# Value projections from seven half-size products, with their sums stored, in a transformer block on one core

## The chip, the cores and the metric

The kernel runs on one core of a Trainium2 chip. The core has a matrix engine (TensorE, PE in the profile; its weight loads are PEld), VectorE (DVE), ScalarE (ACT), GpSimd (POOL) and SyncE (SP), which here only issues transfers, and 16 DMA engines that they share. Each engine works through its own instructions in order. The metric is the time of one execution on the device in microseconds; several runs are taken and their median is compared.

## What is computed

One transformer block in fp32 over 2048 tokens of 512 features. Six rows of 512 numbers (sa, ca, ga, sb, cb, gb) come from a small product and modulate the block.

```python
h = layernorm(x) * (1 + ca) + sa
q, k, v = h @ Q_w + Q_b, h @ K_w + K_b, h @ V_w + V_b     # 16 heads of 128
attn = softmax(causal(q @ k.T / sqrt(128))) @ v
x = x + ga * (sum over heads of attn @ O_w + O_b)
h = layernorm(x) * (1 + cb) + sb
x = x + gb * (64 routed experts, 4 per token + 2 shared experts)(h)
```

The change concerns the values `h @ V_w`, part of the softmax, and where sb, cb and gb are kept until the second half needs them.

## The kernel before

**Layout.** The normalised input lies transposed in four tiles `hTs[j]` of 512 tokens each: 128 partitions, 4 chunks of features, 512 tokens. `Ts[b]` holds four sums and differences of quarters of a pair of such tiles, made once by VectorE (`sum_h`). They serve the query and key projections: `project` computes queries and keys of one head for 1024 tokens from seven half-size products where the plain way has eight (Strassen's scheme, with sums of the weights made by `sum_w`). Its first product is copied by ScalarE, and the other six are added up by VectorE.

**Values.** Two heads make a group; there are eight groups. `make_v` (lines 419 to 434) computes 128 tokens of both heads of a group: four products with a block of `hTs` as the stationary operand and 256 columns of the weights `wv` streaming, summed in one PSUM buffer, and a copy by ScalarE. A group takes 16 such units. The results lie in tiles `v` of 512 tokens by 256 columns.

**Steps.** Attention runs head by head, and each head in five steps, numbered 0 to 4, over pairs of query tiles (`BATCHES`: pair 7; 6; 5 and 0; 4 and 1; 3 and 2). While a step's weighted values are computed, the softmax of the step two further on is made (`softmax_work(n + 2)`), so the softmax work seen in steps 3 and 4 of a head is that of steps 0 and 1 of the next head, the widest ones. For a chunk of up to 1024 scores TensorE writes the products into one of two score buffers in PSUM, VectorE adds the mask where it is needed and takes the maximum, ScalarE takes the exponential, which frees the buffer. A row of more than 1024 scores has two chunks, and a correction factor `fix` joins them. Then the probabilities are divided by their sum: in steps 0 and 1 by VectorE (line 489), in the others by ScalarE (`flush_shares`, line 716). At a step's end `swap` issues the transfers that exchange 32-row blocks of the probabilities (SP's queue, 8 transfers), and VectorE transposes within the blocks (`turn`, line 556) in two halves, at 0.55 and 0.8 of the next step. Only then can TensorE use them as the moving operand of the weighted values (line 574).

**Filling.** Beside these, each step has units that are not tied to it (`fillers`, line 596). In steps 0, 1 and 2 they are five, five and four of the 14 products of the next head's `project`. In steps 3 and 4 they are four and four units of `make_v` for the next group: an even head makes tokens 0 to 1023, an odd head the rest. In the last two heads there is no further group.

**Order.** The schedule is written by hand. `merge` takes the streams of a step (softmax, weighted values, filling), and always emits the next unit of that stream which has emitted the smallest share of its cost; at a tie the stream named first goes first. Marks run an extra piece when a share of the whole has been emitted: the transposes at 0.55 and 0.8, and `sum_w` at 0.3 of step 4, which has ScalarE scale the query weights in place (line 199) and VectorE add and subtract weights (lines 201 to 204). The products of `project`, of `make_v` and of `late_mod` share two PSUM buffers (tag `mm`).

**Modulation rows.** `late_mod` (line 625) computes the row i of the modulation and leaves it on all partitions in one of the tiles ga, sb, gb, cb: ga in head 2, sb in head 4, gb in head 6, cb in head 14. `gate` limits ga and gb with six VectorE operations, in head 2 and head 6.

The attention is followed by the output projection (from about 1690 us), the routing, and the experts (to the end).

Of the kernel before, what the change touches and what calls it, by code (L numbers as in the profile page):

```python
# [9 lines left out]
F32 = mybir.dt.float32  # L10
# [13 lines left out]
def adaln_block_kernel(  # L24
# [49 lines left out]
    silc = const.tile([P, DC, P], F32)  # L74
    ga = const.tile([P, D], F32)
    cb = const.tile([P, D], F32)
    sb = const.tile([P, D], F32)
    gb = const.tile([P, D], F32)
    atd = dram.tile([H, DH, N], F32)
    h2d = dram.tile([N, D], F32)  # L80
    ybd = dram.tile([E * CAP, D], F32)
# [39 lines left out]
    with ExitStack() as att:  # L121
# [41 lines left out]
        def plain(b, j, dst):  # L163

            w = heads[0][b]
            ps = psA.tile([P, 512], F32, name="pqk", tag="mm")
            for k in range(DC):
                nc.tensor.matmul(
                    out=ps,
                    lhsT=w[:, k, :],  # L170
                    rhs=hTs[j][:, k, :],
                    start=(k == 0),
                    stop=(k == DC - 1),
                )
# [19 lines left out]

        sums_w = {}

        def sum_w(hd):
            wq, wk = heads[hd]
            nc.scalar.activation(wq, wq, AF.Identity, scale=scale)
            sw = qkw.tile([P, 4, 2, DH], F32, name="sw")  # L200
            nc.vector.tensor_add(sw[:, 0], wk[:, 0:2, :], wk[:, 2:4, :])
            nc.vector.tensor_sub(sw[:, 1], sw[:, 0], wq[:, 0:2, :])
# [59 lines left out]
        with tc.tile_pool(name="pre", bufs=1) as pre, tc.manual_schedule():  # L262
# [130 lines left out]
                nc.vector.tensor_scalar(silc[:, k, :], ones, sg[:, k : k + 1], None, ALU.mult)  # L393
            plain(1, NB - 1, kts[0, NB - 1])
            plain(0, 3, qts[0, 3])
            sum_w(1)
            sum_h(1)

# [15 lines left out]
        def spare(g):  # L414

            both = [vp.tile([P, 4, HG * DH], F32, name=f"v{at}") for at in free[g]]
            return [b.rearrange("p i d -> p (i d)") for b in both]

        def make_v(g, t):

# [38 lines left out]
        def softmax_tile(hd, s, pr, i, pb):  # L459

            qi = 2 * pr + i
            width = (qi + 1) * P
            nch = (width + SC - 1) // SC
            RB = blocks_of(s)
            r0 = first_block(s, pr) + i * (2 * pr + 1)
            rows = pb[:, : 4 * RB * 32].rearrange("q (b r k) -> q r b k", b=4, k=32)
            cols = pb[:, : 4 * RB * 32].rearrange("q (b r) -> q b r", b=4)  # L470
            box = {}

            def normalise():
                nm, sums = box["nm"], box["sums"]
                rs = smp.tile([P, 2], F32, name="rs")
                if nch == 1:
                    nc.vector.reciprocal(rs[:, 0:1], sums[:, 0:1])
                else:
                    fix = box["fix"]
                    nc.vector.scalar_tensor_tensor(  # L480
                        rs[:, 1:2], sums[:, 0:1], fix, sums[:, 1:2], ALU.mult, ALU.add
                    )
                    nc.vector.reciprocal(rs[:, 1:2], rs[:, 1:2])
                    nc.vector.tensor_mul(rs[:, 0:1], rs[:, 1:2], fix)  # L484
                for n in range(nch):
                    a = (r0 + n * SC // P) * 32
                    b = (r0 + min(width, (n + 1) * SC) // P) * 32
                    if s < 2:
                        nc.vector.tensor_scalar(
                            cols[:, :, a:b], cols[:, :, a:b], rs[:, n : n + 1], None, ALU.mult  # L490
                        )
                    else:
                        shares.append((cols[:, :, a:b], rs[:, n : n + 1]))

            def chunk(n):
                c0 = n * SC
                w = min(SC, width - c0)
                q = qts[hd, qi // 4][:, (qi % 4) * P : (qi % 4 + 1) * P]
                ps = psA.tile([P, SC], F32, name="ps", tag="sc")
                for o in range(0, w, 512):  # L500
                    wo = min(512, w - o)
                    nc.tensor.matmul(  # L502
                        out=ps[:, o : o + wo],
                        lhsT=q,
                        rhs=kts[hd, (c0 + o) // 512][:, :wo],
                        start=True,
                        stop=True,
                    )
# [12 lines left out]
                nc.scalar.activation(  # L521
                    rows[:, r0 + c0 // P : r0 + (c0 + w) // P],
                    ps[:, :w].rearrange("q (r b k) -> q r b k", b=4, k=32),
                    AF.Exp,
                    bias=nm[:, n : n + 1],
                    accum_out=sums[:, n : n + 1],
                )
# [68 lines left out]
        def fillers(hd, s):  # L596

            g = hd // HG
            if s < 3:
                if s == 0 and hd + 1 < H:  # L600
                    ahead.extend(project(hd + 1, 1) + project(hd + 1, 0))
                n = 4 if s == 2 else 5
                out = ahead[:n]
                del ahead[:n]
                return out
            if g + 1 == NG:
                return []
            t0 = (hd % HG) * NP + 4 * (s - 3)
            return [(1024, lambda t=t: make_v(g + 1, t)) for t in range(t0, t0 + 4)]

        ahead = []

# [12 lines left out]
        def late_mod(i, dst):  # L625

            pm = psA.tile([P, D], F32, name="pm", tag="mm")
            for k in range(DC):
                nc.tensor.matmul(
                    out=pm, lhsT=silc[:, k, :], rhs=mods[i][k], start=(k == 0), stop=(k == DC - 1)  # L630
                )
            if i == 4:
                nc.vector.tensor_scalar_add(dst, pm, 1.0)
            else:
                nc.vector.tensor_copy(dst, pm)

        MOD_LOADS = {(2, 0): 2, (4, 0): 3, (6, 0): 5, (14, 0): 4}
        MOD_ROWS = {(2, 2): (2, ga), (4, 2): (3, sb), (6, 2): (5, gb), (14, 3): (4, cb)}


        PLACES = (2, 3, 0, 1)
# [95 lines left out]
        with tc.manual_schedule():  # L737
# [10 lines left out]
            for n, (hd, s) in enumerate(steps):  # L748
# [7 lines left out]
                    load_mod(MOD_LOADS[hd, s], hd // HG)  # L756
                if (hd, s) in MOD_ROWS:
                    fill.append((2048, lambda m=MOD_ROWS[hd, s]: late_mod(*m)))
                if (hd, s) in ((2, 3), (6, 3)):
                    mag = qkw.tile([P, 512], F32, name="p_")  # L760
                    gate(mag, ga if hd == 2 else gb)
                if (hd, s) == (14, 1):
                    fill.insert(2, (0, lambda: load_wo(0)))
                if (hd, s) == (14, 2):
# [30 lines left out]
                if outs:  # L795
                    upto = 8 if hd < H - 1 else (14, 14, 14, 10)[s]
                    fill += outs[:upto]
                    del outs[:upto]
                streams = [weighted_values(hd, s, turned.pop(n)), fill]
                if n + 2 < len(steps):  # L800
                    streams.insert(0, softmax_work(n + 2))
                marks = [(f, lambda i=i: scale_wo(i)) for f, i in WO_SCALES.get((hd, s), ())]
                if s == 4 and hd + 2 < H:
                    marks.append((0.3, lambda: sum_w(hd + 2)))
                if n + 1 < len(steps):
                    marks.append((0.55, lambda: turn(n + 1, 0)))
# [277 lines left out]
    with ExitStack() as ex:  # L1084
# [403 lines left out]
```

## Time and profile before

| | |
|---|---|
| median of three runs | 2420.02 us (2419.19 to 2422.03) |
| the profiled execution | 2419.9 us |
| its span, first to last instruction | 2418.1 us |
| TensorE busy | 2363.9 us |
| VectorE busy | 1511.8 us |
| ScalarE busy | 828.8 us |
| value products (line 427), 1024 records | 240.8 us busy |
| copies of values (line 434), 128 | 46.1 us busy |
| between 98 and 1560 us: TensorE, VectorE, ScalarE busy | 1445.6, 992.7, 625.4 us |

The profile is that of one execution. Each group of instructions has its line, engine, operation, the names of what it writes and reads, its shape, its count, the busy time and the mean length of one, then the idle time of its engine just before, and what ended it. Matrix products are pipelined: the length of one includes the time in which the next has already begun, so what a product costs is read from the distance of starts. An fp32 product shows as two records.

### The profile page before, as it was taken

How to read it: one execution, taken by the hardware profiler on the slowest of the kernel's cores; microseconds unless marked ns; L12 is line 12 of the kernel's file. 1: busy time of each engine (PE TensorE's matmuls, PEld its weight loads, DVE VectorE, ACT ScalarE, POOL GpSimd, SP SyncE). 2: the span in 40 equal slices, each digit the busy share in tenths (PEclk: the TensorE clock that was granted, in tenths of full speed). 3: DMA queues.
4: the chain of work that ended last, by engine and by line, in shares of the span. 5: the costliest groups of instructions: out<-in, count | busy, mean ns of one | idle time of the engine just before them, and what ended most of it. 6: DMA issues, size and time to landing. Idle time of an engine off the chain costs nothing. (4 is left out here: it accounts for less than half of the span.)

```text
span 2418.1 us, 26181 instructions
## 1 busy us (share of the span) xinstructions
PE 2363.9 (98%) x8406; PEld 1500.2 (62%) x8406; DVE 1511.8 (63%) x2878; ACT 828.8 (34%) x1737; POOL 217.8 (9%) x286
## 2 busy tenths in 40 slices
PE   7899999999999999999999999999999999999999
PEld 3566666666666665666666656555444476876743
DVE  5366676676776766767667676764655563654564
ACT  3243443443444444444443444432211221222200
POOL 0000000000000000000000000000000111111073
PEclk9999999999999999999999999999999999999999
DMA  4224544454454443444445444665432368778664
GB/s 140 62 71 116 122 120 108 97 144 102 103 128 108 115 119 95 114 111 103 121 97 124 114 101 120 164 191 140 137 122 87 101 203 250 232 215 244 187 199 153
DMA packets 223681, 325.22 MB, mean 134 GB/s; under 512 B 31876, under 2 KB 138424, under 8 KB 223544
## 3 DMA queue, kind: packets, MB, share of 16 engines
q1 hardware_dynamic: 196664, 252.21, 40.6%
q0 software_dynamic: 17664, 54.54, 7.5%
q10 hardware_dynamic: 9216, 16.78, 1.8%
q8 instruction: 68, 1.11, 0.2%
q14 instruction: 69, 0.57, 0.1%
HBM read 138.86 MB, written 41.94 MB: 75 GB/s over the span
## 5 line engine op out<-in xcount | busy, mean ns | idle before, releaser
L521 ACT ACTIVATE p<-ps,nm 128x1024 f32<-128x1024 f32 (+7 forms) x384 | 332.0, 864 | 879.8 <-DVE nm L519 407.7
L574 PE MATMUL po<-pt,v 128*128 128x256 f32 (+1 forms) x2304 | 571.1, 368 | 16.7 <-DVE pt L556 15.0
L574 PEld LDWEIGHTS po<-pt,v 128*128 128x128 f32 x2304 | 426.6, 190 | 254.5 <-issue 184.1
L502 PE MATMUL ps<-kt,qt 128*128 128x512 f32 (+3 forms) x1280 | 530.9, 531 | 5.8 <-ACT p L521 4.0
L515 DVE TENSOR_REDUCE nm<-ps 128x1 f32<-128x1024 f32 (+7 forms) x384 | 347.5, 908 | 36.1 <-PE ps L502 27.3
L556 DVE STREAM_TRANSPOSE pt<-pt 128x1664 f32<-128x1664 f32 (+2 forms) x160 | 317.8, 1987 | 54.5 <-DMA pt<-p 53.7
L502 PEld LDWEIGHTS ps<-kt,qt 128*128 128x128 f32 x1280 | 233.7, 190 | 172.6 <-issue 137.8
L427 PE MATMUL pv<-wv,hT 128*128 128x256 f32 x1024 | 240.8, 379 | 2.2 <-ACT v L434 2.2
L588 POOL DMA_DIRECT2D atd<-at x128 | 74.3, 584 | 1612.5 <-ACT at L583 1589.4
L427 PEld LDWEIGHTS pv<-wv,hT 128*128 128x128 f32 x1024 | 194.4, 190 | 31.2 <-ACT v L434 3.0
L716 ACT ACTIVATE p<-p,rs 128x1024 f32<-128x1024 f32 (+7 forms) x256 | 200.0, 805 | 6.2 <-DVE rs L484 6.0
L514 DVE TENSOR_TENSOR ps<-ps,causal 128x128 f32<-128x128 f32 x256 | 74.2, 290 | 166.4 <-PE ps L502 163.3
L1058 PE MATMUL pso<-hT,T 128*128 128x512 f32 x384 | 175.4, 602 | 0.0
L217 PE MATMUL pqk<-T,sw 128*128 128x512 f32 x360 | 169.2, 592 | 0.0
L1350 PE MATMUL pse<-wgu,xbT 128*128 128x256 f32 x512 | 121.1, 379 | 0.0
L1058 PEld LDWEIGHTS pso<-hT,T 128*128 128x128 f32 x384 | 70.1, 192 | 72.1 <-issue 71.3
L217 PE MATMUL pqk<-hT,wq 128*128 128x512 f32 x240 | 114.2, 599 | 0.0
L1267 PE MATMUL psd<-wsd,hs 128*128 128x512 f32 x256 | 111.5, 592 | 0.0
L1350 PEld LDWEIGHTS pse<-wgu,xbT 128*128 128x128 f32 x512 | 93.8, 190 | 11.7 <-issue 1.0
L217 PEld LDWEIGHTS pqk<-T,sw 128*128 128x128 f32 x360 | 68.4, 190 | 47.7 <-issue 43.0
L1333 POOL DMA_INDIRECT xb<-h2d,tok x64 | 65.1, 1018 | 302.1 <-PE tpx L1343 273.0
L1345 ACT COPY xbT<-tpx 128x512 f32<-128x512 f32 x64 | 37.4, 586 | 146.0 <-DVE y L1373 54.4
(365 smaller groups left out, 2342.0 us busy)
## 6 DMA issues: line engine op xcount, KB each, us to landing
pt<-p SPq DMA_DIRECT2D x768, 104.0 KB, 2.2
pt<-p SPq DMA_DIRECT2D x256, 124.0 KB, 2.3
pt<-p SPq DMA_DIRECT2D x256, 108.0 KB, 2.2
atd<-at POOLq DMA_DIRECT2D x128, 128.0 KB, 2.2
wgu<-in_L_ffn_Wg_dram SPq DMA_DIRECT2D x64, 256.0 KB, 4.1
wgu<-in_L_ffn_Wu_dram SPq DMA_DIRECT2D x64, 256.0 KB, 4.6
wd<-in_L_ffn_Wd_dram SPq DMA_DIRECT2D x64, 256.0 KB, 3.7
ybd<-y ACTq DMA_DIRECT2D x64, 256.0 KB, 3.8
```

The costliest lines, as they stand in the source:

```text
L217: nc.tensor.matmul(out=ps, lhsT=l[:, k], rhs=r[:, k], start=(k == 0), stop=(k == 1))
L427: nc.tensor.matmul(out=ps, lhsT=hTs[t // 4][:, k, (t % 4) * P : (t % 4 + 1) * P], rhs=wv[:, k].rearrange("p i d -> p (i d)"), start=(k == ...
L502: nc.tensor.matmul(out=ps[:, o : o + wo], lhsT=q, rhs=kts[hd, (c0 + o) // 512][:, :wo], start=True, stop=True,)
L515: nc.vector.tensor_reduce(nm[:, n : n + 1], ps[:, :w], AX.X, ALU.max, negate=True)
L521: nc.scalar.activation(rows[:, r0 + c0 // P : r0 + (c0 + w) // P], ps[:, :w].rearrange("q (r b k) -> q r b k", b=4, k=32), AF.Exp, bias=nm ...
L556: nc.vector.transpose(part, part)
L574: nc.tensor.matmul(out=po if wide else po[:, P:], lhsT=vts[g, kt // 4][:, kt % 4, hh * DH : (hh + 1) * DH], rhs=rows[:, r : r + last + 1 : ...
L588: nc.gpsimd.dma_start(out=atd[hd, :, o * 256 : (o + 1) * 256], in_=at[:, m])
L716: nc.scalar.activation(part, part, AF.Identity, scale=r)
L1058: nc.tensor.matmul(out=ps, lhsT=abs_[pr][:, hd, i * P : (i + 1) * P], rhs=wos[hd // 4][:, hd % 4, :], start=(hd == 0), stop=(hd == H - 1),)
L1267: nc.tensor.matmul(out=ps, lhsT=hsh[b, f][:, i * P : (i + 1) * P], rhs=wsd[:, f, :], start=(f == 0), stop=(f == NHC - 1),)
L1350: nc.tensor.matmul(out=ps, lhsT=xts[e][:, k, :], rhs=weights[e][:, k].rearrange("p i h -> p (i h)"), start=(k == 0), stop=(k == DC - 1),)
```

## The change

Values of groups 1 to 7 are computed by the seven products as queries and keys are. For each head of the pair, `values` makes 1024 tokens of both heads of the group: the two halves of the tokens, of the features and the two heads give the quarters. Each product has four blocks of 128 tokens as the stationary operand, two halves of the feature quarter and 128 columns of one head's weights (or of a stored sum) streaming. ScalarE copies the first product, and VectorE adds up the other six with seven additions. `value_sums` makes four sums of the group's weights, once a group, in step 3 of the even head. Three products run in step 3 and four in step 4. Group 0 stays with `make_v`.

The sums lie in `sgb`, which is the room of the rows sb and gb, and an intermediate result in `cb`. Therefore the rows 3 and 5 are computed in `cb` at the same places as before, written to DRAM (`modd`), and read back into `sgb` at the start of head 14; gb is limited in step 2 of head 15.

Of the two wide tiles of steps 0 and 1, the one made first (i = 1) is normalised by ScalarE; the second stays with VectorE. The scaling of the query weights moves from 0.3 to 0.05 of step 4. In `merge` the filling now stands ahead of the weighted values in every step.

```diff
-    sb = const.tile([P, D], F32)
-    gb = const.tile([P, D], F32)
+    sgb = const.tile([P, 2, D], F32)
+    sb, gb = sgb[:, 0], sgb[:, 1]
+    modd = dram.tile([2, D], F32)
...
+        def scale_w(hd):
+            wq = heads[hd][0]
+            nc.scalar.activation(wq, wq, AF.Identity, scale=scale)
+
         def sum_w(hd):
             wq, wk = heads[hd]
-            nc.scalar.activation(wq, wq, AF.Identity, scale=scale)
...
+        def value_sums(g):
+            wv = groups[g]
+            s = sgb.rearrange("p a (j k d) -> p (a j) k d", j=2, k=2)
+            nc.vector.tensor_add(s[:, 0], wv[:, 0:2, 1], wv[:, 2:4, 1])
+            nc.vector.tensor_sub(s[:, 1], s[:, 0], wv[:, 0:2, 0])
+            nc.vector.tensor_sub(s[:, 2], wv[:, 0:2, 0], wv[:, 0:2, 1])
+            nc.vector.tensor_sub(s[:, 3], wv[:, 2:4, 0], s[:, 1])
+            return s
+
+        def values(g, b, s):
...
+            def product(l, r):
+                ps = psA.tile([P, 4, DH], F32, name="pv", tag="mm")
+                for n in range(4):
+                    for k in range(2):
+                        nc.tensor.matmul(
+                            out=ps[:, n], lhsT=l[:, k, n * P : (n + 1) * P], rhs=r[:, k],
+                            start=(k == 0), stop=(k == 1),
+                        )
+                return ps
...
+            def first():
+                box["p"] = qkw.tile([P, 512], F32, name="p_").rearrange("p (t d) -> p t d", t=4)
+                nc.scalar.copy(box["p"], product(hTs[i][:, 0:2], wv[:, 0:2, 0]))
+
+            def second():
+                nc.vector.tensor_add(u, box["p"], product(T[:, 1], s[:, 1]))
+
+            def third():
+                place(i)
+                nc.vector.tensor_add(of(i, 1), u, product(T[:, 2], s[:, 2]))
+
+            def fourth():
+                place(j)
+                ps = product(T[:, 0], s[:, 0])
+                nc.vector.tensor_add(of(j, 1), of(i, 1), ps)
+                nc.vector.tensor_add(of(j, 0), u, ps)
+
+            def fifth():
+                nc.vector.tensor_sub(of(i, 1), of(i, 1), product(T[:, 3], wv[:, 2:4, 1]))
+
+            def sixth():
+                nc.vector.tensor_add(of(j, 0), of(j, 0), product(hTs[j][:, 2:4], s[:, 3]))
+
+            def seventh():
+                nc.vector.tensor_add(
+                    of(i, 0), box["p"], product(hTs[i][:, 2:4], wv[:, 2:4, 0])
+                )
...
-                    if s < 2:
+                    if s < 2 and i == 0:
                         nc.vector.tensor_scalar(
...
-            t0 = (hd % HG) * NP + 4 * (s - 3)
-            return [(1024, lambda t=t: make_v(g + 1, t)) for t in range(t0, t0 + 4)]
+            if s == 3:
+                if hd % HG == 0:
+                    sums_v[0] = value_sums(g + 1)
+                behind.extend(values(g + 1, hd % HG, sums_v[0]))
+            out = behind[: s]
+            del behind[: s]
+            return out
...
+            if i in (3, 5):
+                nc.sync.dma_start(out=modd[i // 5 : i // 5 + 1, :], in_=dst[0:1, :])
...
-        MOD_ROWS = {(2, 2): (2, ga), (4, 2): (3, sb), (6, 2): (5, gb), (14, 3): (4, cb)}
+        MOD_ROWS = {(2, 2): (2, ga), (4, 2): (3, cb), (6, 2): (5, cb), (14, 3): (4, cb)}
...
-                if (hd, s) in ((2, 3), (6, 3)):
+                if (hd, s) in ((2, 3), (15, 2)):
...
+                if (hd, s) == (14, 0):
+                    nc.sync.dma_start(out=sgb, in_=modd.partition_broadcast(P))
...
-                streams = [weighted_values(hd, s, turned.pop(n)), fill]
+                streams = [fill, weighted_values(hd, s, turned.pop(n))]
...
                 if s == 4 and hd + 2 < H:
+                    marks.append((0.05, lambda: scale_w(hd + 2)))
                     marks.append((0.3, lambda: sum_w(hd + 2)))
```

More of the change, by code (lines that the diff above doesn't have):

```diff
@@ L395, in adaln_block_kernel @@
             plain(0, 3, qts[0, 3])
+            scale_w(1)
             sum_w(1)
@@ L417, in spare, with place, of @@
             return [b.rearrange("p i d -> p (i d)") for b in both]
+        def value_sums(g):
[7 more added lines that the diff above has]
+        def values(g, b, s):
+            i, j = 2 * b, 2 * b + 1
+            T = Ts[b]
+            wv = groups[g]
+            u = cb.rearrange("p (t d) -> p t d", t=4)
+            box = {}
+            def product(l, r):
[7 more added lines that the diff above has]
+                return ps
+            def place(j):
+                vts[g, j] = vp.tile([P, 4, HG * DH], F32, name=f"v{vplace[g][j]}")
+            def of(j, hh):
+                return vts[g, j][:, :, hh * DH : (hh + 1) * DH]
+            def first():
[19 more added lines that the diff above has]
+                )
+            return [(1024, f) for f in (first, second, third, fourth, fifth, sixth, seventh)]
@@ L607, in fillers @@
                 return []
-            t0 = (hd % HG) * NP + 4 * (s - 3)
-            return [(1024, lambda t=t: make_v(g + 1, t)) for t in range(t0, t0 + 4)]
+            if s == 3:
[5 more added lines that the diff above has]
+            return out
         ahead = []
+        behind = []
+        sums_v = {}
         mods = {}
```

## The prediction

> **What bounds the kernel now.** I began with the page: busy time of each engine, then the waits of TensorE, then the stretches of the attention.
>
> The page's first lines:
>
> ```profile
> span 2418.1 us, 26181 instructions
> ...
> PE 2363.9 (98%) x8406; PEld 1500.2 (62%) x8406; DVE 1511.8 (63%) x2878; ACT 828.8 (34%) x1737; POOL 217.8 (9%) x286
> ```
>
> TensorE is busy 98% of the span, VectorE 63%. A busy share alone can hide stalls, so I took the waits of TensorE between 150 and 1560 us, where the value products of groups 1 to 7 lie (who waited for whom: total us, times, longest):
>
> ```profile
> PE po L574 <- DVE pt L556: 7.0, 9, 1.6
> PE ps L502 <- ACT p L521: 3.0, 6, 0.9
> ```
>
> Ten microseconds in 1410: TensorE sets the pace there, and a change in time has to come from its instructions or from new waits of these two kinds. The stretches of one odd head (head 7, steps 3 and 4, then head 8, step 0) show what the others have left; columns are the stretch, its length, busy PE, PEld, DVE, ACT, POOL, the granted clock, DMA share, GB/s:
>
> ```profile
> 872.10:890.30 18.20, 18.20 (x74) 13.24 (x73) 10.45 (x15) 7.56 (x18) 1.07 (x2) 1.00 0.65 166
> 890.30:910.40 20.10, 18.84 (x80) 14.13 (x78) 14.19 (x24) 6.95 (x18) 1.28 (x2) 1.00 0.49 115
> 910.40:930.40 20.00, 20.00 (x65) 12.02 (x65) 15.04 (x29) 8.85 (x22) 1.22 (x2) 1.00 0.43 102
> ```
>
> The clock is full. VectorE has 8 us free in step 3 and 6 in step 4; ScalarE has 11 or more.
>
> **Part 1: seven products for eight.** Removed, for groups 1 to 7 (group 0 keeps the old way): 7 x 64 products of 256 columns. Each fp32 product is two records of the profile (the line has x1024 for 8 x 64). How far apart records start, I read from the timeline of TensorE (start, length, instruction, count):
>
> ```profile
> 902.56 1.89 PE L427 MATMUL pv<-wv,hT 128*128 128x256 f32 x8
> 904.29 0.59 PE L574 MATMUL po<-pt,v 128*128 128x256 f32 x2
> ```
>
> Eight records of 256 columns take 904.29 - 902.56 = 1.73 us, 0.216 each (the mean of 379 ns includes overlap). Removed: 896 x 0.216 = 193.5 us.
>
> Added: 7 x 14 = 98 products, each of 4 token blocks x 2 halves of 128 columns, so 16 records, each with a stationary block of its own. The columns fall to 7/8, the records rise from 896 to 1568, and so do the weight loads. Nothing before runs 16 such records on end; the nearest rows:
>
> ```profile
> 1759.02 0.60 PE L890 MATMUL tp<-ident,h 128*128 128x128 f32 x4
> 1759.46 3.60 PE L1058 MATMUL pso<-hT,T 128*128 128x512 f32 x8
> 1762.89 1.00 PE L899 MATMUL pl<-wr,h2T 128*128 128x64 f32 x8
> ```
>
> Four 128-column transposes, each with another block, start every 0.109 us (0.44 for four). Eight fp32 records of only 64 columns, each with another block, start 0.111 to 0.112 apart after the first, though their columns would need half of that: this is the pace of loading a 128x128 fp32 block. Here a rule speaks against the change: the Trainium skill ("TensorE: Matmul & The Clock Gate", LDWEIGHTS) puts a load at the number of stationary columns / 1.2 ns, however few columns then stream, 107 ns for 128. With 256 columns a load has 216 ns to hide in, with 128 none to spare. By the rule the stream still decides, 0.109: 1568 x 0.109 = 170.9, a gain of 22.6 us. By the row of 64 columns loading decides, 0.112: 1568 x 0.112 = 175.6, a gain of **17.9 us**. I take the row, as its records are fp32 products with distinct blocks; 22.6 stays as the good end. The bad end, loads not hidden at all (190 ns each, the PEld row): 298 us, 104 lost; the 64-column run excludes it nearly.
>
> The gain lies in step 3, which goes from four units of 1.73 to three of 1.79 (-1.5 us); step 4 keeps four (+0.25).
>
> **Part 2: the results move from ScalarE to VectorE.** ScalarE loses 16 copies of 368 ns a group and gets two of 128x512. VectorE gets for each of 14 heads seven additions of 128x512 from PSUM; the same form in the query products takes 668 to 688 ns:
>
> ```profile
> L244 DVE TENSOR_TENSOR qt<-qt,pqk 128x512 f32<-128x512 f32 x30 | 20.3, 678 | 0.0
> L489 DVE TENSOR_SCALAR p<-p,rs 128x1024 f32<-128x1024 f32 x80 | 58.8, 752 | 2.3
> L716 ACT ACTIVATE p<-p,rs 128x1024 f32<-128x1024 f32 x80 | 91.5, 1143 | 6.2 <-DVE rs L484 6.0
> DVE sw L202 <- ACT wq L199: 38.3, 15, 7.5
> ```
>
> (the last is of the waits). Two of the additions fall in step 3, five in step 4: 1.4 and 3.4 us. The sums of the weights are four adds of 128x256 at 0.42, 1.7 us in step 3 of every even head.
>
> Against that, the normalisation of the first wide tile goes to ScalarE: in step 3 two chunks of 1024, in step 4 1024 + 768 (0.75 + 0.61, overlapping: 1.3 to 1.5 us a step off VectorE; 2.3 and 2.1 us onto ScalarE, which has 11 free and puts them behind an exponential, ahead of the next chunk's, whose maximum comes later anyway). And scaling the query weights at 0.05 of step 4 instead of just ahead of the sums takes away VectorE's wait for it, 2.3 us in the heads I looked at.
>
> Step 3: 10.45 - 1.4 + 1.4 + 0 or 1.7 = 10.5 to 12.2 us, in 16.7 of TensorE. Step 4: 14.2 - 1.3 + 3.4 = 16.3 in 18.84 + 0.25 = 19.1, with 2.3 less waiting. Both fit; 85% in step 4 leaves little. In step 4 the last addition stands ahead of the second block transpose. From the end of the seventh product VectorE needs 0.69 (addition) + 2.24 (transpose) + 0.27 + 0.82 + 0.16 (mask, maximum), ScalarE 0.79 (exponential of 640), 4.97 us, until the score buffer is free. TensorE in the new order has 0.43 + 1.08 + 0.65 in this step, then 0.22, the head's first query product 1.72 and 0.43, 4.53 us, before it needs that buffer. So a new wait of **0.4 us in each of 14 heads, 6 us**. Bounds: none, if VectorE's stated lengths overlap by their 0.08 as its rows do; 1.4 each where its queue is a microsecond behind, 20 us.
>
> **Part 3: fill in front of the weighted values.** At a step's start TensorE now has a product of 1.7 us to do before the weighted values ask for the transposed probabilities. Every wait of the 7.0 above is at most 1.6 us, so 7.0 goes; of the one at the start of head 0 (5.1 us, at 108) 1.7 is covered. Counted again from the end of the seventh product, VectorE has the second transpose done after 0.69 + 2.24 = 2.9 us, and TensorE asks for it after 0.43 + 1.08 + 0.65 + 0.22 + 1.72 = 4.1: the cover holds with 1.2 to spare. Gain **8.7**, from 0 to 8.7.
>
> **Part 4: rows kept in DRAM.** Two rows go out through SP's queue in heads 4 and 6, and one load of 512 KB comes back at the start of head 14; behind them in SP's queue are the block swaps of the probabilities, which are issued at a step's end, microseconds later; a load of 512 KB lands in 6.6 us by the page. The gate of the last row (six VectorE operations) moves from head 6 to step 2 of head 15, where no projections run any more. The first addition of head 4 step 3 waits for the row's transfer, about 2 us, issued some 6 us before. All 0, at worst 2 us.
>
> **Sum.** -17.9 + 6 - 8.7 = -20.6. The profiled execution took 2419.9 us (span 2418.1 and 1.8 around), the median shown is 2420.0: the same. 2420 - 20.6 = 2399; I say **2400**.
>
> **Rivals.**
> *A, as above (0.74)*: 2400, its own range 2391 to 2413.
> *B, VectorE becomes the bound in step 4 (0.13)*: its items there sum to 16.3, and in order it also waits 1.4 + 1.2 us for ScalarE's correction factors and up to 2.1 for the swaps to land: 21.0 against TensorE's 19.1, 1.9 a head over and 0.4 of part 2 besides. For: step 4 of head 7 has all these waits. Against: they are waits it has time for while ahead, and the longest (2.1) now runs beside the sixth product. If all of it comes through, 14 x 2.3 = 32: 2420 - 17.9 - 1.7 + 32 = 2432, slower. It decides from 1.4 us a head.
> *C, given back (0.11)*: the waits for the score buffer are 1.0 to 1.4 a head, 14 to 20 us, or the waits for transposes stay: 2412 to 2420.
> *D, weight loads not hidden (0.02)*: 2524.
>
> A change under 0.2% (4.8 us) is what a measurement of this kernel can't tell from none. Faster: A and most of C, 0.80; same: the rest of C and a little of B, 0.07; slower: 0.13. The range takes in the rule's 22.6 with all of part 3 and no new wait (2389) and C's bad end (2420).
>
> **What would show it.** Right: value records of 128 columns 0.109 to 0.112 apart, step 3 1.5 us shorter, step 4 as long as before; VectorE's total up by some 33 us (98 additions at 0.68 and 28 sums at 0.42, less 48 x 0.752 + 16 x 0.614 of normalising); TensorE's waits on transposes near nothing between 150 and 1560; waits on the exponential up by a few us. Wrong: records 0.12 apart or more, waits of value products for VectorE (its additions not done), step 4 or step 0 of the next head longer than now by over a microsecond.

## The result, and the profile after

The changed kernel took 2426.05 us (median of 20 runs, 2418.85 to 2435.89), the kernel before, on the same chip, 2421.91 (20 runs, 2418.81 to 2423.57): a ratio of **1.0021** (95% interval 1.0012 to 1.0030). It is slower by 0.2%, where 2400 and faster was predicted. The profiled execution took 2432.7 us, one of the longer ones. The kernel before took 2420 us beside some of the experiments below and 2432 beside others, so each ratio is to the kernel before as it ran beside that experiment, on the same chip.

The first lines of the page, which answer to those of before:

```profile
span 2430.9 us, 27582 instructions
...
PE 2357.7 (97%) x9078; PEld 1507.3 (62%) x9078; DVE 1540.5 (63%) x2940; ACT 864.2 (36%) x1703; POOL 217.9 (9%) x286
...
PE 59%; SPq 15%; DVE 10%; DMA 5%; issue 5%; ACT 3%; POOL 0%; DVEq 0%; ACTq 0%; POOLq 0%
SPq L616 14%; PE pqk L222 11%; PE ps L572 9%; PE po L644 9%; PE pso L1140 6%; PE pst L1287 5%; PE pse L1432 5%; PE psd L1349 5%; DVE pt L626 4%; DMA pt<-p 3%; PE psy L1453 2%; PE psg L1203 2%; PE psb L769 2%; DVE nm L585 2%; PE tpx L1425 1%
```

TensorE is busy for 6 us less, VectorE for 29 more, and the span is 12.8 longer. The last two lines are the chain that ended last, by engine and by line. Its second entry is SP's queue with 15%, nearly all of it on line 616, the transfers of the block swap. This cannot be compared with the kernel before: there the chain could be followed back only to 1576 us, so its shares sum to 35% and leave out most of the attention.

The waits of TensorE between 150 and 1560 us (who waited for whom: total us, times, longest), after:

```profile
PE ps L572 <- ACT p L591: 23.2, 20, 1.5
PE po L644 <- DVE pt L626: 7.8, 8, 2.2
```

They were 3.0 and 7.0. The waits on transposes, which were to go, are all there, and the waits for the score buffer have grown by 20 us. Nearly all of them stand at the start of step 0: the score product waits there in each of the heads 1 to 15, 0.9 to 1.5 us, and in nine of them the weighted values just ahead of it wait too, 0.5 to 2.2 us. The three stretches shown of the kernel before, after:

```profile
872.10:890.30 18.20, 18.20 (x97) 13.92 (x96) 9.91 (x16) 7.52 (x14) 1.07 (x2) 1.00 0.45 109
890.30:910.40 20.10, 19.12 (x111) 15.14 (x109) 15.92 (x27) 7.74 (x15) 1.28 (x2) 1.00 0.69 168
910.40:930.40 20.00, 17.87 (x49) 9.84 (x50) 12.75 (x25) 9.38 (x20) 1.21 (x2) 0.91 0.42 102
```

TensorE has no idle time in the first, 1 us in the second, 2.1 in the third, where the granted clock (after POOL's column) is 0.91 too.

To find where it goes I cut each trace at the first weighted-value record of every step. The table gives mean us per step over ten heads that compute no modulation row (1, 3, 5, 7 to 13), worked out from the starts of the records; "alone" is the sum of the distances at which the records follow each other when nothing is waited for.

| | step 0 | 1 | 2 | 3 | 4 | head |
|---|---|---|---|---|---|---|
| before | 22.54 | 20.53 | 18.09 | 19.19 | 17.43 | 97.78 |
| after | 24.23 | 20.44 | 18.15 | 17.64 | 17.92 | 98.38 |
| after, alone | 22.33 | 19.97 | 18.06 | 17.46 | 16.83 | 94.65 |

Step 3 is shorter by 1.55 us, as predicted. Step 0 of the next head gives back 1.7 of it, and step 4 another 0.5. Over heads 1 to 13 the trace of after is longer by 7.5 us (1289.8 for 1282.3), over heads 14 and 15 by 7.1, nearly all of it in their steps 0. Some 9 of these 14.6 us are not waits but a lower clock behind them (last section).

### The profile page after: what moved, and what is told of

Read it like the earlier page. It is cut to its first block, busy times and chain, and to the rows that moved or that the text cites. A ratio compares the mean times of both kernels' runs of the same rounds, so it can differ in the third digit from the quotient of the medians.

```text
span 2430.9 us, 27582 instructions
## 1 busy us (share of the span) xinstructions
PE 2357.7 (97%) x9078; PEld 1507.3 (62%) x9078; DVE 1540.5 (63%) x2940; ACT 864.2 (36%) x1703; POOL 217.9 (9%) x286
## 4 chain that ended last, share of the span: by engine, by line
PE 59%; SPq 15%; DVE 10%; DMA 5%; issue 5%; ACT 3%; POOL 0%; DVEq 0%; ACTq 0%; POOLq 0%
SPq L616 14%; PE pqk L222 11%; PE ps L572 9%; PE po L644 9%; PE pso L1140 6%; PE pst L1287 5%; PE pse L1432 5%; PE psd L1349 5%; DVE pt L626 4%; DMA pt<-p 3%; PE psy L1453 2%; PE psg L1203 2%; PE psb L769 2%; DVE nm L585 2%; PE tpx L1425 1%
## 5 line engine op out<-in xcount | busy, mean ns | idle before, releaser
L644 PE MATMUL po<-pt,v 128*128 128x256 f32 (+1 forms) x2304 | 567.5, 369 | 14.1 <-DVE pt L626 12.6
L572 PE MATMUL ps<-kt,qt 128*128 128x512 f32 (+3 forms) x1280 | 539.6, 538 | 29.1 <-ACT p L591 27.0
L795 ACT ACTIVATE p<-p,rs 128x1024 f32<-128x1024 f32 (+3 forms) x320 | 266.1, 860 | 6.5 <-DVE rs L554 6.3
L1140 PEld LDWEIGHTS pso<-hT,T 128*128 128x128 f32 x384 | 70.1, 192 | 72.1 <-issue 71.3
L222 PEld LDWEIGHTS pqk<-T,sw 128*128 128x128 f32 x360 | 68.4, 190 | 54.1 <-issue 50.2
L447 PEld LDWEIGHTS pv<-sgb,T 128*128 128x128 f32 x672 | 81.6, 192 | 8.1 <-issue 6.7
L1349 PEld LDWEIGHTS psd<-wsd,hs 128*128 128x128 f32 x256 | 48.6, 190 | 59.0 <-issue 58.1
```

Of the source, the lines that this page charges most:

```text
L222: nc.tensor.matmul(out=ps, lhsT=l[:, k], rhs=r[:, k], start=(k == 0), stop=(k == 1))
L572: nc.tensor.matmul(out=ps[:, o : o + wo], lhsT=q, rhs=kts[hd, (c0 + o) // 512][:, :wo], start=True, stop=True,)
L644: nc.tensor.matmul(out=po if wide else po[:, P:], lhsT=vts[g, kt // 4][:, kt % 4, hh * DH : (hh + 1) * DH], rhs=rows[:, r : r + last + 1 : ...
L795: nc.scalar.activation(part, part, AF.Identity, scale=r)
L1140: nc.tensor.matmul(out=ps, lhsT=abs_[pr][:, hd, i * P : (i + 1) * P], rhs=wos[hd // 4][:, hd % 4, :], start=(hd == 0), stop=(hd == H - 1),)
L1349: nc.tensor.matmul(out=ps, lhsT=hsh[b, f][:, i * P : (i + 1) * P], rhs=wsd[:, f, :], start=(f == 0), stop=(f == NHC - 1),)
```

## What sets the pace now: the swap

The DMA issues of the page (what is written and read, queue, count, KB each, median us from issue to landing), and below them the durations of one issue (min/median/max ns) from the rows of line 616:

```profile
pt<-p SPq DMA_DIRECT2D x768, 104.0 KB, 2.2
pt<-p SPq DMA_DIRECT2D x256, 124.0 KB, 2.3
pt<-p SPq DMA_DIRECT2D x256, 108.0 KB, 2.2
```
```profile
L616 SPq DMA_DIRECT2D pt<-p x1280: 507/592/2240, 80.5 to 1690.4; - x183
```

A step's swap is 1280 / 80 = 16 transfers (not 8, as the description of the kernel above has it). SP issues them one after another, 0.592 us each and about 0.64 from start to start, so the last is issued some 9.6 us after the first and lands 2.3 us later. Only then can VectorE transpose the second half. Here is one such round in the timeline of after (start, length, instruction, count, idle time ahead and its releaser), SP first, then VectorE, then ScalarE, then SP's next round:

```profile
1192.89 10.15 SPq L616 DMA_DIRECT2D pt<-p  x16
```
```profile
1203.61 0.69 DVE L483 TENSOR_TENSOR v<-p__7160,pv 128x512 f32<-128x512 f32 x1
1204.86 2.25 DVE L626 STREAM_TRANSPOSE pt<-pt 128x1984 f32<-128x1984 f32 x1 [0.56 <-DMA pt<-p]
1207.03 0.27 DVE L584 TENSOR_TENSOR ps<-ps,causal 128x128 f32<-128x128 f32 x1
1207.33 0.82 DVE L585 TENSOR_REDUCE nm<-ps 128x1 f32<-128x640 f32 x1
1208.18 0.16 DVE L589 TENSOR_TENSOR nm<-nm 128x1 f32<-128x1 f32 x1
1209.54 0.22 DVE L550 SCALAR_TENSOR_TENSOR rs<-sums,fix 128x1 f32<-128x1 f32 x1 [1.20 <-ACT fix L601]
...
1210.18 1.22 DVE L559 TENSOR_SCALAR p<-p,rs 128x1024 f32<-128x1024 f32 x2
```
```profile
1208.44 0.79 ACT L591 ACTIVATE p<-ps,nm 128x640 f32<-128x640 f32 x1 [2.33 <-DVE nm L589]
```
```profile
1211.54 10.91 SPq L616 DMA_DIRECT2D pt<-p  x16
```

The issues end at 1203.04, the last transfer has landed at 1204.73, and VectorE, idle for 0.56 us, begins the transpose at 1204.86. The addition of the seventh product (line 483) was done before, so it is not what is waited for. Behind the transpose come, in VectorE's order, the mask and the maximum of the last chunk of scores, then ScalarE's exponential, the sum, the normalising, and only now the next swap can be issued: a ring of 1211.54 - 1192.89 = 18.65 us, in which VectorE, ScalarE, SP and the transfers take turns. In the kernel before, the same two rounds begin 18.77 apart (1187.03 and 1205.80). The change did not touch this ring, and it shortened TensorE's step 3, just ahead. For all heads together: the two rounds from the swap for a head's step 4 to that for step 1 of the next head take 38.3 us before and 38.8 after, on average over the 14 such places.

The exponential frees the score buffer that TensorE asks for in step 0. TensorE, in the same stretch:

```profile
1205.80 1.88 PE L222 MATMUL pqk<-hT,wq 128*128 128x512 f32 x4
1207.52 0.59 PE L644 MATMUL po<-pt,v 128*128 128x256 f32 x2
1209.37 1.98 PE L572 MATMUL ps<-kt,qt 128*128 128x512 f32 x4 [1.26 <-ACT p L591]
```

Here the filling in front (line 222) covers the transpose: the weighted values at 1207.52 do not wait. But the score product right behind them needs the exponential of a chunk whose maximum stands behind the same transpose on VectorE. Call this **theory R**, the ring: the time is set by the swap's landing, and neither the order nor TensorE's work moves it. Its rivals: **V**, VectorE's new additions (what the prediction feared in part 2 and rival B); **O**, the new order itself makes the wait.

## The experiments

Means of steps and stretches come from the profiled execution of each, as in the table above.

### Undoing one part at a time

**The values of before in the changed kernel** (a_makev; order, normalising and early scaling stay):

```diff
-            if s == 3:
-                if hd % HG == 0:
-                    sums_v[0] = value_sums(g + 1)
-                behind.extend(values(g + 1, hd % HG, sums_v[0]))
-            ...
+            t0 = (hd % HG) * NP + 4 * (s - 3)
+            return [(1024, lambda t=t: make_v(g + 1, t)) for t in range(t0, t0 + 4)]
```

> The changed kernel with the values made by eight full products and ScalarE's copies again; the order, ScalarE's normalising and the early scaling stay. R: 17.9 us more of TensorE work falls into time that was waited out: 2414 to 2424, no slower than the changed kernel by more than 2. V: VectorE is rid of 78 us of additions and sums, so the waits go as well: 2408 to 2414. If the change's saving of TensorE work is real at the end: 2436 or more.

Measured: 0.9979 (0.9966 to 0.9992). Of 2420 us that is 2415 (2412 to 2418), inside R's range, but the interval reaches into V's (2408 to 2414), so this run does not part the two. It does show where the saving went: TensorE's waits are 11.6 us for 31.0, so 19 us of waiting go where 17.9 us of work come back.

**The order of before in the changed kernel** (a_order):

```diff
-                streams = [fill, weighted_values(hd, s, turned.pop(n))]
+                streams = [weighted_values(hd, s, turned.pop(n)), fill]
```

> The changed kernel with the weighted values again ahead of the fill. R: the same end of the ring is waited for one instruction earlier, by the weighted values instead of the score product; time within 4 us of the changed kernel's, 2420 to 2430. O: the wait of 1.7 us in 14 heads goes and none comes instead: 2400 to 2408.

Measured: 1.0040 (1.0021 to 1.0059), in R's range. O falls: the old order does not bring the time down. The wait changes its name; its waits of TensorE:

```profile
PE po L644 <- DVE pt L626: 24.7, 14, 3.1
PE ps L572 <- ACT p L591: 3.3, 5, 1.1
```

24.7 and 3.3 for 7.8 and 23.2: the weighted values now wait for the transpose, and the score product behind them mostly no longer has to.

**Without the last two additions** (a_light, beside a_again, the changed kernel once more). ScalarE only copies the sixth and seventh products, and part of the sum of the values is left out:

```diff
-                nc.vector.tensor_add(of(j, 0), of(j, 0), product(hTs[j][:, 2:4], s[:, 3]))
+                nc.scalar.copy(of(j, 0), product(hTs[j][:, 2:4], s[:, 3]))
...
-                nc.vector.tensor_add(of(i, 0), box["p"], product(hTs[i][:, 2:4], wv[:, 2:4, 0]))
+                nc.scalar.copy(of(i, 0), product(hTs[i][:, 2:4], wv[:, 2:4, 0]))
```

> The changed kernel unaltered, for comparison on the same chip as the three others: between 0.2% slower and 0.6% slower than the kernel before.

> The changed kernel with the sixth and seventh value products only copied by ScalarE instead of added by VectorE, so a part of the sum is left out of two quarters of the values; VectorE has 1.4 us less in step 4, and no wait for a product ahead of either transpose. V: the waits fall by 1 to 1.4 us in 14 heads: 14 to 20 us below the changed kernel. R: the second transposes begin when the last transfer has landed, as before; 0 to 5 us below it.

Measured: 1.0017 (1.0007 to 1.0027) and 1.0016 (1.0005 to 1.0027), the same. V falls: VectorE has 1.4 us less to do and starts the transpose no earlier, 12.54 us after the first issue of the swap for step 0 on average over the ten heads, for 12.52 in a_again. In its timeline:

```profile
1208.08 2.25 DVE L624 STREAM_TRANSPOSE pt<-pt 128x1984 f32<-128x1984 f32 x1 [1.21 <-DMA pt<-p]
```

The idle time ahead of it, 0.56 in the changed kernel, is 1.21: VectorE only waits longer for the DMA. The two rounds of the swap, 38.3 us before and 38.8 after, are 38.6 in a_again and 38.4, 38.5 and 38.5 in a_makev, a_order and a_light: with more work on TensorE, another order or less on VectorE they stay what they were.

ScalarE's normalising and the early scaling were not undone alone. Together with the order they are worth 0.3 us a head once the ring is cut (b_diag against d_makev below).

### Shortening the issue: three ways that failed

If SP's 16 issues are the link to cut, half of them could go through another queue. The second half of the swap by GpSimd, in the changed kernel (a_pool) and in that of before (b_pool), then by ScalarE, `nc.scalar` in the same place (a_act, b_act):

```diff
-                    nc.sync.dma_start(
+                    (nc.sync if half == 0 else nc.gpsimd).dma_start(
```

> The changed kernel, with the second half of each step's block swap (8 of 16 transfers) issued from GpSimd's queue instead of SP's. Theory R (ring): the swap is 16 issues of 0.63 us one after another on SP, 10 us, and a landing, transposes, mask, maximum, exponential and normalisation close a ring of about 19.4 us a step that steps 3 and 4 (17.6 and 17.0 us of TensorE work) cannot undercut; with the chain cut by 4 to 5 us the waits at the head boundaries go, and the time falls to 2394 to 2403 us. Theory V (VectorE's additions hold up the transposes): no more than 5 us, 2419 to 2426. Theory O (fill ahead of the weighted values lays the score buffer's chain bare): as V.

> The kernel before, with the same half of the block swap on GpSimd's queue. R: step 4 loses its 0.7 us a head over its TensorE work, some 10 us in 14 heads: 2408 to 2413 us. V and O, which put the trouble into the change alone: 2418 to 2422. The gap between this kernel and the changed one with the same edit is by R the 18 us of TensorE work saved, less a few us: 8 to 18.

> The changed kernel with the second half of each block swap (8 of 16 transfers) issued from ScalarE's queue, where an issue took 0.33 us in the experts. R (ring): the last issue ends about 5 us after the first instead of 10, the second transposes start some 8 us after the first issue instead of 12.4, and the waits of steps 3, 4 and 0 go: 20 to 30 us below the changed kernel unaltered. V (VectorE's additions): within 5 us of it. If ScalarE, which now waits for the normalisation and issues for some 3 to 5 us a step, holds up the exponentials, steps 0 to 2 grow by the time lost.

> The kernel before with the same edit. R: 8 to 14 us below the kernel before; the changed kernel with the edit is then 10 to 18 us faster than this one, the saving of its value products. V: within 3 us of the kernel before.

Measured: a_pool 1.0326 (1.0307 to 1.0346), b_pool 1.0478 (1.0460 to 1.0495), a_act 1.0852 (1.0797 to 1.0906), b_act 1.1031 (1.1011 to 1.1051). All far slower, where R had expected all four to be faster; only a_act's expectation allowed that ScalarE might be held up. The trace says why. With GpSimd, over heads 1 to 13, it takes 15.3 and 14.1 us from the first issue of the swaps for steps 0 and 4 to the start of their second transpose, for 12.5 and 12.5 in the changed kernel: the issues end sooner, but VectorE waits longer for the transfers (148.5 us between 150 and 1560, for 68.4), and the ring is longer. With ScalarE, its own waits between 150 and 1560 us, and one of them in its timeline:

```profile
ACT p L591 <- DMA pt<-p: 444.9, 64, 9.3
```
```profile
1195.92 6.16 ACTq L616 DMA_DIRECT2D pt<-p  x8
1202.28 1.11 ACT L591 ACTIVATE p<-ps,nm 128x1024 f32<-128x1024 f32 x1 [6.39 <-DMA pt<-p]
```

The releaser's name misleads. ScalarE is not waiting for a landing, it is issuing: its eight transfers take it 6.1 us a swap, 392.6 us of the 444.9, during which it computes nothing, and the next exponential starts 0.2 us (median) after the last issue. The landing is longer too (3.1 us through SP and 3.2 through ScalarE, for 2.2). Here the Trainium skill ("DMA: Bandwidth & Descriptors", Issuing engines are not separate DMA queues) says that several issuing engines save only the sequencer's issue time, "usually small relative to the DMA itself". In this case the issue time is the large part, 16 x 0.64 = 10.2 us against a landing of 2.2, and splitting it still lost. What the failed runs do show is that the time follows the ring: per head, a_pool's five stretches from first issue to second transpose sum to 70.1 us for 65.2, 4.9 more, and its heads 1 to 13 take 1350.6 us for 1289.8, 4.7 more a head.

**The second transpose later**, at 0.92 of the step and not at 0.8 (a_turn, b_turn), so that VectorE does other work until the transfers land:

```diff
-                    marks.append((0.8, lambda: turn(n + 1, 1)))
+                    marks.append((0.92, lambda: turn(n + 1, 1)))
```

> The changed kernel with the second block transposes at 0.92 of a step instead of 0.8, which puts them behind the mask and maximum of a step's last score chunk on VectorE in steps 3 and 4. R (ring): the last chunk's maximum and exponential no longer wait for the landing of the swap; the ring loses about 3 us (first issue to next first issue 19.3 to about 16.5) and TensorE's 17.6 and 17.0 set the pace of steps 3 and 4; the score buffer is free in time. 20 to 30 us below the changed kernel: 2394 to 2405 where the kernel before takes 2421. V (VectorE's amount of work): the same work in another order, within 5 us of the changed kernel.

> The kernel before with the same edit. R: its waits on the transposes at the start of step 0 (0.7 us in 14 heads) go at most in part, as TensorE has no product in front of the weighted values: 3 to 10 us below the kernel before. The difference to the changed kernel with the edit is the saving of value products, 12 to 18 us.

Measured: 1.0041 (1.0026 to 1.0055) and 1.0491 (1.0473 to 1.0508). R had expected 20 to 30 us less in a_turn and 3 to 10 in b_turn, and missed both. In a_turn step 0 falls to 22.47 us, but step 1 rises from 20.4 to 22.2 and step 4 to 18.5: a later transpose makes the next link later. The wait was moved, not removed. In b_turn all five steps are longer, by 0.9 to 2.7 us; why by so much more was not tried.

### Taking transfers out of the ring

Of the 16 blocks four stay in their own partitions (d = 0). GpSimd, busy 9% of the span, can copy them itself, and SP has 12 to issue; in the changed kernel (a_diag) and in that of before (b_diag):

```diff
+                    if d == 0:
+                        nc.gpsimd.tensor_copy(
+                            pt[32 * a : 32 * (a + 1), a * w : (a + 1) * w],
+                            pb[32 * a : 32 * (a + 1), a * w : (a + 1) * w])
+                        continue
                     nc.sync.dma_start(
```

> The changed kernel with the 4 of 16 swap transfers that stay in their partitions made as copies by GpSimd, which has nothing else to do there; SP issues 12. R: the last issue comes 2.5 us earlier, so the second transposes begin about 10 us after the first issue instead of 12.4, if GpSimd's copies are done by then: the waits of 1.7 and 0.7 us a head go, 20 to 30 us below the changed kernel. If the copies take longer than 2 us each, the chain gets longer by the excess in each of the five steps, and so does the time. V: within 5 us.

> The kernel before with the same edit. R: 8 to 13 us below it (its 0.7 us in step 4 and 0.4 in step 1 of 14 heads); the changed kernel with the edit is 8 to 18 us faster than this.

Measured: a_diag **0.9874** (0.9857 to 0.9890; 2391.17 us), b_diag 0.9944 (0.9928 to 0.9961; 2406.74 us). The issue of a swap takes 7.7 us for 10.4 on average, and the two rounds 37.1 us for 38.8. The copies, and what is left of TensorE's waits in a_diag:

```profile
L617 POOL COPY pt<-p 32x832 f32<-32x832 f32 (+2 forms) x320 | 292.9, 915 | 139.1 <-DVE p L559 103.7
```
```profile
PE ps L572 <- ACT p L591: 9.7, 16, 0.7
```

The 31 us of waits are 9.7. With the ring shortened in both kernels the changed one is 15.6 us faster (R: 8 to 18); without, it is 4 slower: this is theory R shown. Against the changed kernel's 1.0021 the cut is worth some 35 us, more than the 20 to 30 that R had said. It also makes a kernel faster than either.

### With the ring cut, the prediction's parts once more

Three kernels, each a_diag with one of the edits above: the old order (d_order), the last two additions left out, with part of the sum (d_light), the old values (d_makev).

> The kernel with the four diagonal blocks copied by GpSimd (2391.2 us), with the weighted values ahead of the filling again, as before the change. Theory R (the score product in step 0 waits for the end of the second transpose plus about 2.1 us, whichever stands first): 2388 to 2394, the wait only moves from the score product to the weighted values. Part 3 of the prediction (the filling in front covers a wait that the old order would show): 1.7 us a head or more come back, 2398 or above.

> The kernel with the four diagonal blocks copied by GpSimd, in which the sixth and seventh products are only copied by ScalarE; their additions are left out, so part of the values is not summed. Part 2 of the prediction (the last addition ahead of the second transpose holds up the score buffer): the 9.7 us of waits on the exponential in step 0 vanish, 2380 to 2385. Theory R (what is left of them is still the swap's landing): 2388 to 2394.

> The kernel with the four diagonal blocks copied by GpSimd, with the values made by the old eight products; the order, ScalarE's normalising and the early scaling of the query weights stay. Theory R and part 1 of the prediction: the saving of 17.9 is gone, and with it the 9.7 us of waits that the longer step 3 hides: 2391.2 + 17.9 - 9 = 2400, up to 2409 if the waits stay. If the seven products themselves were worth nothing: 2391.

And one with nothing left out (e_late): the seventh product is copied by ScalarE, and the addition comes at the start of the next step 0, behind the transpose and its softmax.

```diff
-                nc.vector.tensor_add(
-                    of(i, 0), box["p"], product(hTs[i][:, 2:4], wv[:, 2:4, 0])
-                )
+                nc.scalar.copy(of(i, 0), product(hTs[i][:, 2:4], wv[:, 2:4, 0]))
+                later.append(lambda: nc.vector.tensor_add(of(i, 0), of(i, 0), box["p"]))
...
+                if s == 0 and later:
+                    later.pop()()
```

> The kernel with the four diagonal blocks copied by GpSimd, complete, with only the addition of the seventh product moved: ScalarE copies the product, and VectorE adds the stored first product at the start of the next step 0, behind the second transpose and its softmax. Part 2 of the prediction (the addition ahead of the transpose, 0.69 us, holds up the score buffer by as much): 0.69 of the 0.88 us that step 0 is longer goes, 14 heads, 2380 to 2384. If the sixth addition and not the seventh is what holds it up, or the moved addition comes back as another wait: 2388 to 2394.

| | ratio (interval) | median us | before beside it | step 0 | 3 | 4 | head | heads 1 to 13 |
|---|---|---|---|---|---|---|---|---|
| b_diag | 0.9944 (0.9928 to 0.9961) | 2406.74 | 2420.47 | 22.54 | 19.19 | 16.97 | 97.19 | 1274.0 |
| d_makev | 0.9902 (0.9886 to 0.9919) | 2396.59 | 2420.62 | 22.37 | 19.19 | 16.84 | 96.87 | 1269.6 |
| d_order | 0.9892 (0.9875 to 0.9908) | 2395.01 | 2420.62 | 22.54 | 17.64 | 17.79 | 96.44 | 1265.0 |
| a_diag | 0.9874 (0.9857 to 0.9890) | 2391.17 | 2420.47 | 23.25 | 17.64 | 17.02 | 96.44 | 1265.0 |
| d_light | 0.9835 (0.9818 to 0.9851) | 2380.34 | 2420.62 | 22.37 | 17.64 | 17.02 | 95.56 | 1253.5 |
| e_late | 0.9835 (0.9822 to 0.9849) | 2392.28 | 2432.24 | 22.39 | 17.64 | 17.02 | 95.58 | 1253.7 |

Of the expectations, part 2's came out in d_light (2380 to 2385) and, as a ratio, in e_late; d_order lies 1 us above R's range, and d_makev between its two (2400 and more; 2391). What follows:

- *The order* is worth nothing in heads 1 to 13: a_diag and d_order take 1265.0 both; 0.75 us moves between steps 0 and 4. The 3.8 us between their medians lie elsewhere, and their intervals overlap.
- *The last additions* cost 0.88 us a head (96.44 for 95.56), once the ring is cut, and it is the seventh: e_late moves that one alone and has it all back. By its ratio it is the fastest complete kernel here, 1.65% below before.
- *The seven products* without that cost: d_light less d_makev, 95.56 - 96.87 = -1.31 us a head, and -1.29 in e_late, where nothing is left out.

In a_diag the chain of part 2 can be seen at work: the addition waits for its product, not the transpose for a DMA.

```profile
1182.84 0.69 DVE L483 TENSOR_TENSOR v<-p__7160,pv 128x512 f32<-128x512 f32 x1 [0.55 <-PE pv L447]
1183.45 2.24 DVE L632 STREAM_TRANSPOSE pt<-pt 128x1984 f32<-128x1984 f32 x1
```

## Why the prediction was wrong

**What bounds the kernel.** "TensorE sets the pace there" held for the kernel before, and it was read as if nothing stood right behind it. VectorE's waits for the swap were in the trace, 39.0 us between 150 and 1560 (68.4 after), and only rival B used them. The swap was taken as one transfer, "up to 2.1 for the swaps to land" (rival B), and never as 16 issues in a row.

**Part 1, the seven products: right.** The records follow each other at 0.111 to 0.112 us, the value taken from the row of 64-column records and not the 0.109 of the good end; step 3 is 1.55 us shorter (said: 1.5). The saving of 17.9 us, 1.28 a head over 14, is 1.31 a head where it can show (d_light against d_makev).

**Part 2, the results on VectorE: right in its mechanism, wrong in size, because a link was missing.** The chain from the seventh product's end was put at 4.97 us and TensorE's at 4.53, a wait of 0.4. In a_diag, where the chain does bind, the score product starts at 1187.96, 5.12 us after the addition began, and the addition begins 0.2 us after the end of the product by the distance of records: 5.32 for 4.97, 0.6 of wait in the profile and 0.88 us a head by moving it. In the changed kernel itself step 0 grew by 1.7 us, and the additions had no part in it (a_light): the transpose stood waiting for the swap, which the chain had left out. So where 0.4 us a head had been put, 1.7 came. VectorE's total rose by 28.7 us (said: 33).

**Part 3, the filling in front: the step that failed outright.** "Every wait of the 7.0 above is at most 1.6 us, so 7.0 goes." The 1.7 us of cover are there, and 7.8 us of waits are left for 7.0, as TensorE now comes to each head's end earlier and the swap does not. And the cover was counted as gain without asking what stands behind it: the next score product needs the exponential of a chunk whose maximum follows the same transpose. Gain 0 for 8.7: heads 1 to 13 take 1289.8 us with the new order and 1290.8 with the old (a_order), 1265.0 with either once the ring is cut (d_order, a_diag).

**Part 4** stays at nothing: no wait of TensorE in either list is for a modulation row, and in heads 14 and 15 the waits that grew are the same two.

**The sum.** -17.9 + 6 - 8.7 was -20.6. What happened in heads 1 to 13 of the profiled run: a saving of 1.55 in step 3, then +1.69 in step 0 and +0.49 in step 4 on average. The saving came and the waits took it all: the runs whose mean clock was 0.996, as before, took 2419 us. The other 7 us up to the median of 2426 go with a lower clock, which the prediction had at full and put no term on. Rival C ("given back", 1.0 to 1.4 a head, or the transposes' waits stay) named the place and had the two as alternatives; both came, at 1.7 a head, so the result lies past C's end at 2420. Rival B (2432) had the sign, and half of its reason holds: VectorE's own work is excluded by a_light, but the last item of its sum, VectorE waiting for the swaps to land, is what grew.

## What to carry to other kernels

Before TensorE's work is cut, time the ring beside it: from the first issue of a step's transfers to the first issue of the next step's, every engine in turn, and look whether any link in it waits for TensorE. If none does and the ring is as long as the step, the saving comes back as waits, under whatever name stands first in the queue, and the cure is a shorter ring (fewer issues, a link taken off it), not less work on TensorE. A row of many small transfers is costed by its issues, not by one landing.

## What the runs showed of the hardware that was not expected

**The clock can fall to half after short waits that lie close together.** At the start of head 8, the third stretch shown above, TensorE waited 1.08, 0.51 and 1.52 us within 6 us; no single wait was long. From its timeline in the changed kernel:

```profile
910.50 0.49 PE L572 MATMUL ps<-kt,qt 128*128 128x128 f32 x2 [1.08 <-ACT p L591]
...
913.22 0.70 PE L644 MATMUL po<-pt,v 128*128 128x256 f32 x2 [0.51 <-DVE pt L626]
915.44 3.27 PE L572 MATMUL ps<-kt,qt 128*128 128x512 f32 x4 [1.52 <-ACT p L591]
```

The four records at 915.44 take 3.27 us; the four at 1209.37 above, after a single wait, took 1.98. The granted clock in these stretches (the column after POOL's count):

```profile
912.00:915.40 3.40, 1.41 (x4) 0.30 (x2) 2.34 (x4) 1.22 (x4) 0.00 (x0) 1.00 0.00 0
915.40:918.50 3.10, 3.06 (x4) 1.28 (x5) 2.26 (x7) 1.21 (x5) 1.21 (x2) 0.59 0.21 71
```

The Trainium skill ("TensorE: Matmul & The Clock Gate", Part 1) ties the half clock to an idle window of about 3.4 us; here it followed waits that sum to 3.1 us, with work between them, and in a_order a single wait of 2.07 us (granted clock 0.50 from 716.5 to 719.8). The trace of after has such stretches of half clock at 315 and 916 us (3.4 us each) and at 1503 and 1605 (6.8 each), all behind waits at the start of a step 0, and the kernel before has the full clock there. TensorE is busy for 18.1 of these 20.5 us; by that, an estimate, they cost some 9 of the 12.8 us by which the profiled execution is longer. Of the 20 runs those with a mean clock of 0.996 took 2418.9 to 2419.1 us, those with 0.990 and 0.989 took 2430.7 and 2435.9.

The sum of the waits does not decide it: in the same trace head 1 waits 1.91 and 1.52 us within 4 us and keeps the clock at 1.00, and a_turn waits 47.2 us in all between 150 and 1560 us without one stretch of half clock there. What does decide it, and whether the waits cause every such fall, was not tried.

**The same transfers, issued through two queues at once, land later**: 3.1 us through SP's and 3.2 through ScalarE's beside it, for 2.2 through SP's alone. Why was not tried either.
